# Two-layer graph network on one core: sweep 2 rearranged (halves, one more tile place, a fixed order of TensorE's steps), weights requested later, features transposed in pairs of blocks

## The chip, the cores and the metric

The kernel runs on one core of a Trainium2 chip. The metric is the device time of one execution in microseconds (us); the times of the kernel before are the median of three runs. A profile is one execution recorded by the hardware profiler: its span goes from the first to the last instruction of the program, and the time of that same execution is somewhat longer than its span.

## The reference

`x` is 4096 x 64, `adj` is 4096 x 4096 with about 0.8% of its entries set and the diagonal added. Two layers follow each other, each with a layer norm and a ReLU in front and a residual around it:

```python
h = relu(layernorm(x))                       # layer 0
for k in range(2):                           # two hops
    agg = adj @ h
    h = tanh(concat([agg, h], axis=1) @ W[k])
x = x + h
h = relu(layernorm(x))                       # layer 1
support = h @ weight
mask = adj != 0
rank = cumsum(mask, axis=1); deg = rank[:, -1:]
k = minimum(deg, 100)
pos = rank - (deg - k)
w = mask * where(pos > 0, 0.5 ** (k - pos), 0)
x = x + (w @ support + bias)
```

So `adj` is multiplied three times by a 4096 x 64 matrix: twice in float32 by its values, and once by weights 0.5^(k - pos) that follow from the running count of non-zero entries in each row.

## The kernel before, in words

The 4096 nodes are four chunks of eight blocks of 128. `adj` arrives transposed. TensorE works on tiles of 128 x 1024 entries: one source block against one chunk of destinations. Since the features are 64 wide, the two 512-wide halves of a tile go to two column halves of the array at the same time (`agg_pair`, L302). Each float32 matmul leaves two records in the trace, so one such tile is four records.

**Sweep 1** (L479 on) reads all of `adj` once, in pairs of blocks of 1 MB, and does hop 1, all four chunks of destinations one after the other; chunk 0 comes first, with an order of its own (L568). While a tile lies in SBUF, VectorE and ScalarE also turn it into running counts, one byte an entry, that stay in SBUF as `codes` (L267 to L287). `features_T` (L316) transposes a chunk's normalized features, `weighted` (L226) multiplies them with the upper half of W[0] ahead of the hop, `own_share` (L240) with the lower half. One array `hx` holds both, features in its first 64 columns and weighted features in the last 64. `at_step` says after which tile of chunk 0 each of these calls stands. As soon as a chunk has its hop-1 result, it is put in the place of its features, and the tiles of later rows that touch it serve hop 2 as well: those tiles are multiplied twice (`fused`). These 1 MB tiles are counted from 0 in the order of their loads (0 to 15 belong to chunk 0), the half-MB tiles of sweep 2 from 0 again. Of row 1, the pairs with blocks 3 and 1 are moved behind its first EARLY = 7 pairs. SyncE issues all loads; each waits for its place to come free (`places`, `busy`, `load`, L509).

**Sweep 2** (`sweep2`, L931) loads the remaining 72 half-MB tiles of `adj` a second time, for the part of hop 2 that sweep 1 could not do (`hop`, L976; L987 for chunk 0), in the order of `plan`: chunk 2, chunk 3, the rest of chunk 2, chunk 1, chunk 0. When a chunk's hop-2 sum is there, `finish_x2` (L679) takes it through the product with W[1] (`py`, L697), Tanh, residual, layer norm and ReLU, and writes the layer-1 features as a high and a low part in `feat` (L743, L744). Layer 1 is 128 units (J, g, n): source chunk J, destination chunk g, block n. A unit needs the features of chunk J and one 128 x 1024 tile of weights, which `convert` (L790) makes from the codes: on ScalarE with one Exp (L810), or on VectorE with two operations through a buffer `bits` (L802, L805). `layer1` (L856) then does two full-width matmuls (L870). Sums of a (J, g) that are not `kept` in PSUM are added to `parts` in SBUF (`evict`, L887). `finish_out` multiplies a destination chunk with the layer-1 weight (`pto`, L918), adds bias and residual and writes it out.

The order in which the engines get their instructions is fixed when the program is built, by a planner in `sweep2`: it keeps a clock for each engine with estimated durations (`use`), lets the converters run ahead of TensorE by `lead`, and at each point chooses whether the next thing on TensorE is a unit or a tile, by which tiles it believes to have landed and how many units can run. `n_late` = 56 units are held back until the tiles are through. The places of weights come from `space`: buffers that are free again, such as ring pairs that need no more tiles (`consumed`, `KEEP` = 4 of five ring pairs go on), and the codes of a (J, g) that is done (`pair_space`). Tiles of sweep 2 have the ten places of the ring and, once, the place of `hx0`.

Each engine works through its own queue in order and waits on semaphores.

Of the kernel before, what the change touches and what calls it, by code (L numbers as in the profile page):

```python
# [44 lines left out]
def gnn_kernel(  # L45
# [50 lines left out]
    hxs = [place([P, CB, 2 * D], F32, f"hx{q}", "hx") for q in range(NCH)]  # L96
    at = lambda b: hxs[b // CB][:, b % CB, :]
# [129 lines left out]
    def weighted(I):  # L227

        v = by_t(flat(pre1[:, chunk(I), :]))
        pt = (one if I % 2 else two)(name="pg")  # L230
        for t in range(TC):
            nc.tensor.matmul(  # L232
                pt[:, t * P : (t + 1) * P].rearrange("p (c e) -> p c e", c=NC),
                v[:, t // 2, t % 2, :], wz[:, :, 0, 0, :],
                start=True, stop=True, skip_group_check=True,
            )
        nc.scalar.copy(
            as_nodes(hxs[I][:, :, D:]), pt.rearrange("p (t c e) -> p t c e", t=TC, c=NC)
        )

    def own_share(I, po=None):

        h = flat(pre1[:, chunk(I), :])
        keep = po is not None
        po = po if keep else two(name="po")
        paired(po, (lambda c: wz[:, c, 0, 1], lambda c: h), last=not keep)
        if not keep:
            nc.scalar.copy(h, po)
# [69 lines left out]

    def features_T(I):

        pt = (two if I % 2 else one)(name="ph")
        for t in range(TC):
            for c in range(NC):
                nc.tensor.matmul(
                    pt[c * D : (c + 1) * D, t * P : (t + 1) * P],
                    hxs[I][:, c * TC + t, :D], ident, start=True, stop=True, skip_group_check=True,
                )
        nc.scalar.copy(
            by_t(flat(pre1[:, chunk(I), :])), pt.rearrange("q (u v p) -> q u v p", u=2, v=2)
        )  # L330
# [49 lines left out]
    def finish_first(acc, quads):  # L380
# [4 lines left out]
        def x1_half(c):  # L385
# [14 lines left out]
            for h in range(2):  # L400
                nc.scalar.copy(
                    as_nodes(hxs[0][:, :, :D])[:, 2 * h : 2 * h + 2, c], nodes(banks[h])[:, :, 0, c]
                )

        def hop1(b):
            for c in range(NC):
                nc.tensor.matmul(  # L407
                    G[c * D : (c + 1) * D, :], at(b)[:, :D], part_of(quads[c, b // 4], b),
# [33 lines left out]
    def finish_row(I, acc):  # L442
# [9 lines left out]
        take(hxs[I][:, :, :D], banks, 0)  # L452
# [26 lines left out]
    def sweep1():  # L479
        b0 = NB - CB // 2  # L480
        load_x(NCH - 1)
        first = ln_relu(hxs[-1][:, CB // 2 :, :D], pre1[:, b0:, :])
        NQ = NB // 4
        order1 = {I: [*range(NB - 1, 0, -2)] for I in range(1, NCH)}
        EARLY = 7
# [44 lines left out]
        MARKS1 = (6, 9, 12, 15)  # L530
        marks0 = {1: 2, 2: 4, 7: 8, 10: 13, 11: 15}
        F, G, S = features_T, weighted, own_share
        at_step = {1: [(F, 3), (F, 2)], 2: [(G, 3), (G, 2)], 4: [(S, 2)], 5: [(F, 0)], 6: [(G, 0)], 7: [(F, 1)], 8: [(G, 1)], 9: [(S, 3)], 10: [(S, 1)]}
        to_count = [*range(8), *range(9, 16), 8]

        for k in range(2 * NQ):
            _, (c, q) = units[k]
            if k == 0:
                load(1)
                load_x(2)  # L540
                copies = load_weights()
                next(copies)
                load(2)
                load_x(1)
                load(3)
                load_x(0)
            if k == 1:
                next(copies)
# [3 lines left out]
            if k == 0:  # L552
                rest = ln_relu(hxs[-1][:, : CB // 2, :D], pre1[:, NB - CB : b0, :])
                for g in (2, 1, 0):
                    lns[g] = ln_relu(hxs[g][:, :, :D], pre1[:, chunk(g), :])
                ends = []
                for n in (CB // 2, 0):
                    v = slice(n, n + CB // 2)
                    ends.append(ln_relu(hxs[2][:, v, :D], pre1[:, 2 * CB :, :][:, v]))
                for g in (first, first, rest, first, rest, ends[0], rest, ends[0], ends[1], ends[0], ends[1]):  # L560
                    next(g, None)
# [4 lines left out]
            for b in (4 * q + n for n in (2, 3, 0, 1)):  # L566
                h = b % 2
                nc.tensor.matmul(  # L568
                    low0[c][h * D : (h + 1) * D, :], at(b)[:, :D], part_of(a, b),
# [3 lines left out]
            order_ = {0: (1, 2), 1: (1, 'n', 1), 2: (0,), 3: (0, 0)}.get(k, ("n", "n") if k == 7 else ("n",))  # L573
# [24 lines left out]
        for k in range(2 * NQ, len(units)):  # L598
# [16 lines left out]
            for r in (1, 0):  # L615
                g = b - 1 + r
                last = n == HB - 1 and r == 0
                agg_pair(acc[1], at(g)[:, D:], a[:, r], g == NB - 1, last)
# [485 lines left out]
```

## Time and profile before

| what | value |
|---|---|
| time, median of 3 runs (lowest, highest) | 341.48 us (340.38, 344.35) |
| the profiled execution: time, span | 343.04 us, 341.3 us |
| TensorE matmul busy | 329.6 us |
| VectorE busy | 280.4 us |
| ScalarE busy | 190.5 us |
| moved by DMA, mean rate | 108.47 MB, 318 GB/s |
| granted TensorE clock | 1.000 |
| stages, by TensorE: first tile; tile 6; end of hop 1 (first tile of sweep 2 after it); first unit; tiles of sweep 2 through; last matmul | 6.9; 26.6; 196.7; 223.7; 301.6; 337.7 us |

A line of instructions in the profile names the source line, the engine, the operation, what is written and read, the shape and the number of instructions; then come busy time, the mean of one in ns, and idle time before them with what ended it. In the timeline a line begins with start and duration in us and ends with the idle time ahead of it in brackets. PE is TensorE, PEld its weight loads, DVE VectorE, ACT ScalarE, POOL GpSimd, SP SyncE. The clock column of the profile stays at full speed throughout.

### The profile page before, as it was taken

The numbers are of one execution on the slowest core, as the hardware profiler recorded it, in microseconds if no ns is written. First come the engines' busy times: TensorE is split into PE (matmuls) and PEld (weight loads), VectorE is DVE, ScalarE is ACT, GpSimd is POOL, SyncE is SP. The second block draws the span as 40 slices with busy tenths as digits, with TensorE's granted clock in tenths as the row PEclk, the third lists the DMA queues.
The fourth block names the chain that finished last, engine by engine and source line by source line (L and its number), as shares of the span: only waits on it lengthen the run. The fifth ranks groups of instructions, "written<-read, shape, count | busy, mean of one in ns | idle before, by whom it ended". The sixth has DMA issues, their size and how long they took to land.

```text
span 341.3 us, 4305 instructions
## 1 busy us (share of the span) xinstructions
PE 329.6 (97%) x1578; PEld 150.1 (44%) x1578; DVE 280.4 (82%) x439; ACT 190.5 (56%) x199; POOL 23.5 (7%) x21
## 2 busy tenths in 40 slices
PE   8699999999999999999999999899999999998995
PEld 2354433433334333343333433143454656466885
DVE  4869999999999999999969683779456799889933
ACT  2493673285444590233480424037468999969990
POOL 2340000000000000000000000312003000003000
PEclk9999999999999999999999999999999999999999
DMA  7999999999999889976999999999996946500012
GB/s 265 420 423 420 424 415 427 418 422 421 421 418 423 371 321 419 356 270 219 381 361 292 324 356 411 409 409 407 407 396 237 344 151 219 198 17 0 2 52 71
DMA packets 22404, 108.47 MB, mean 318 GB/s; under 512 B 2416, under 2 KB 3824, under 8 KB 14320
## 3 DMA queue, kind: packets, MB, share of 16 engines
q1 hardware_dynamic: 22384, 108.21, 81.3%
q8 instruction: 12, 0.20, 0.2%
q14 instruction: 8, 0.07, 0.1%
HBM read 107.15 MB, written 1.05 MB: 317 GB/s over the span
## 4 chain that ended last, share of the span: by engine, by line
PE 82%; DMA 12%; DVE 3%; ACT 1%; SPq 0%; issue 0%
PE acc_low L302 25%; PE acc L302 20%; PE accl L870 16%; PE acc L987 6%; DMA codes<-in_adjA_dram 5%; DMA ring<-in_adjA_dram 5%; PE acc L568 4%; PE pto L918 2%; PE acc L407 2%; DMA wb<-in_weights_dram 2%; PE pt L370 2%; PE py L697 1%; PE acc_low L568 1%; PE po L215 1%; PE pg L232 1%; PE pt L396 1%
## 5 line engine op out<-in xcount | busy, mean ns | idle before, releaser
L810 ACT ACTIVATE weights<-codes 128x1024 fp32r<-128x1024 uint8 x91 | 87.6, 1044 | 7.0 <-PE accl L870 4.4
L302 PE MATMUL acc<-ring,hx 128*64 128x512 f32 x352 | 86.3, 597 | 1.7 <-DMA ring<-in_adjA_dram 1.7
L302 PE MATMUL acc_low<-ring,hx 128*64 128x512 f32 x264 | 65.5, 593 | 0.0
L870 PE MATMUL accl<-weights,feat 128*128 128x512 f32 x254 | 62.9, 399 | 1.5 <-DVE feat L744 1.5
L870 PEld LDWEIGHTS accl<-weights,feat 128*128 128x128 f32 x254 | 46.2, 188 | 20.7 <-ACT weights L810 7.1
L302 PEld LDWEIGHTS acc<-ring,hx 128*64 128x64 f32 x352 | 23.6, 136 | 52.5 <-issue 39.8
L471 DVE TENSOR_TENSOR codes<-codes,after 128x2048 uint16<-128x2048 uint16 x32 | 38.2, 1218 | 0.1
L302 PEld LDWEIGHTS acc_low<-ring,hx 128*64 128x64 f32 x264 | 19.0, 137 | 37.5 <-issue 37.4
L267 ACT ACTIVATE codes<-ring 128x2048 int8<-128x2048 f32 x10 | 19.1, 1908 | 27.7 <-DMA ring<-in_adjA_dram 27.6
L283 DVE TENSOR_SCALAR mbuf<-ring 128x2048 uint8<-128x2048 f32 x28 | 34.2, 1221 | 0.0
L268 ACT ACTIVATE codes<-codes 128x2048 uint8<-128x2048 int8 x17 | 32.5, 1910 | 0.5
L276 DVE TENSOR_SCALAR cnt<-codes 128x1024 uint16<-128x1024 uint16 (+1 forms) x80 | 29.9, 373 | 2.7
L275 DVE TENSOR_TENSOR codes<-mbuf,cnt 128x1024 uint16<-128x1024 uint16 (+1 forms) x51 | 30.0, 588 | 1.9
L805 DVE TENSOR_SCALAR weights<-bits 128x1024 fp32r<-128x1024 f32 x36 | 25.9, 719 | 6.1 <-PE accl L870 2.2
L302 PE MATMUL acc_low<-codes,hx 128*64 128x512 f32 x120 | 27.8, 593 | 0.0
L802 DVE TENSOR_SCALAR bits<-codes 128x1024 uint32<-128x1024 uint8 x36 | 24.9, 691 | 0.8
L718 POOL TENSOR_TENSOR pre<-pre,wb 128x512 f32<-128x512 f32 x4 | 5.4, 1360 | 270.3 <-DVE xc L197 260.6
L987 PE MATMUL acc<-ring,hx 128*64 128x512 f32 x96 | 21.9, 598 | 0.0
L283 DVE TENSOR_SCALAR mbuf<-codes 128x2048 uint8<-128x2048 f32 x17 | 20.7, 1220 | 0.0
L202 POOL TENSOR_TENSOR s<-s,half 128x8 f32<-128x8 f32 (+1 forms) x10 | 16.9, 1688 | 18.2 <-DVE s L201 18.2
L275 DVE TENSOR_TENSOR codes<-codes,cnt 128x1024 uint16<-128x1024 uint16 (+1 forms) x24 | 13.9, 580 | 3.7 <-ACT codes L268 2.4
L302 PEld LDWEIGHTS acc_low<-codes,hx 128*64 128x64 f32 x120 | 8.5, 137 | 17.0 <-issue 17.0
(98 smaller groups left out, 275.4 us busy)
## 6 DMA issues: line engine op xcount, KB each, us to landing
ring<-in_adjA_dram SPq DMA_DIRECT2D x74, 512.0 KB, 7.9
ring<-in_adjA_dram SPq DMA_DIRECT2D x37, 1024.0 KB, 8.2
codes<-in_adjA_dram SPq DMA_DIRECT2D x26, 1024.0 KB, 17.7
pre<-in_x_dram SPq DMA_DIRECT2D x4, 256.0 KB, 6.9
xres<-in_x_dram SPq DMA_DIRECT2D x4, 256.0 KB, 8.7
out_dram<-o SPq DMA_DIRECT2D x3, 256.0 KB, 2.5
out_dram<-o SPq DMA_DIRECT2D x2, 128.0 KB, 2.2
wb<-in_weights_dram SPq DMA_DIRECT2D x1, 192.0 KB, 6.3
```

Of the source, the lines that this page charges most:

```text
L267: nc.scalar.activation(sign, tile_of(I, a), AF.Sign)
L268: nc.scalar.activation(m, sign, AF.Square, scale=float((FLAG - 1 + 0.25) ** 0.5))
L275: nc.vector.tensor_tensor(q, m, cnt, op=ALU.add)
L276: nc.vector.tensor_scalar(cnt, q, 0x7F7F, None, op0=ALU.bitwise_and)
L283: nc.vector.tensor_scalar(m, tile_of(I, a), 0.0, float(FLAG - 1), op0=ALU.not_equal, op1=ALU.mult)
L302: nc.tensor.matmul(acc[c * D : (c + 1) * D, :], src, a[:, c * C : (c + 1) * C], start=first, stop=last,)
L471: nc.vector.tensor_tensor(q, q, a[:, None, :].to_broadcast([P, 4, CW // 2]), op=ALU.subtract)
L802: nc.vector.tensor_scalar(state["bits"], q, float(ZERO), ONE, op0=ALU.subtract, op1=ALU.mult)
L805: nc.vector.tensor_scalar(w, state["bits"].bitcast(F32), 2.0 ** (127 - LOW), None, op0=ALU.mult)
L810: nc.scalar.activation(w, q, AF.Exp, scale=LN2, bias=BIAS)
L870: nc.tensor.matmul(sums[g][:, c, :], feats[J][:, k, :], w[:, c * C : (c + 1) * C], start=first, stop=last,)
L987: nc.tensor.matmul(accs[0][c * D : (c + 1) * D, :], at(b + h)[:, :D], tiles[n + c][2][:, h * C : (h + 1) * C], start=(0, b + h) == firsts[ ...
```

## The change

It has three groups of edits.

*Start and sweep 1.* The load of the layer weights is issued after that of tile 1 instead of before it, and their copy into place (`W`) is a call in `at_step`; the pieces of the layer norms stand in another order on VectorE (`'frffrarbaab'`, `order_`). `hx` is split into `hx` (features) and `gx` (weighted features), each with two chunks in one array. Chunks 1 to 3 are transposed by four 128 x 128 transposes of two adjacent blocks each, instead of eight matmuls with the identity; `weighted` and `own_share` follow the new order of columns. `own_share(3)` moves from step 9 to 8, `weighted(1)` from 8 to 9, `own_share(1)` from 10 to 11. EARLY is 10 instead of 7. Row 1 gets one more mark on ScalarE, one settle moves from (2, 9) to (3, 2), and the marks of two tiles of chunk 0 move.

*Places.* `gx1` is a twelfth place for tiles of sweep 2, requested ahead of the ring's; `gx0` takes the part that `hx0` had. Three instead of four ring pairs go on, and the pairs in `tile_pairs` become places for tiles when their codes are used. `bits` gets two buffers from unit 32 on, and VectorE can convert two units in one go.

*Sweep 2.* `plan` takes two blocks of chunk 2 ahead of chunk 3 instead of four. `finish_x2` works in two halves for chunks 3 and 0 (`SPLIT`), with the copy of the sum shared between ScalarE and VectorE; a unit waits for the half of the features that it reads, and the blocks of a unit group are ordered by halves. `kept`, `order` and `in_low` change which sums stay in PSUM: three (J, g) are spilled instead of eight. The choice by estimated landing is replaced by `steps2`: after so many tiles, so many units.

```diff
-    hxs = [place([P, CB, 2 * D], F32, f"hx{q}", "hx") for q in range(NCH)]
+    hxs, gxs = (
+        [v[:, q] for r in range(NCH // 2) for v in [place([P, 2, CB, D], F32, f"{n}{r}", n)] for q in range(2)]
+        for n in ("hx", "gx")
+    )
...
     def features_T(I):
...
+        if I:
+            for j in range(CB // 2):
+                nc.tensor.transpose(pair(pt, j), pair(flat(hxs[I]), j), ident)
+            nc.scalar.copy(h, pt)
+            return
...
-        EARLY = 7
+        EARLY = 10
...
-        at_step = {1: [(F, 3), (F, 2)], 2: [(G, 3), (G, 2)], 4: [(S, 2)], 5: [(F, 0)], 6: [(G, 0)], 7: [(F, 1)], 8: [(G, 1)], 9: [(S, 3)], 10: [(S, 1)]}
+        at_step = {1: [(W, 0), (F, 3), (F, 2)], 2: [(G, 3), (G, 2)], 4: [(S, 2)], 5: [(F, 0)], 6: [(G, 0)], 7: [(F, 1)], 8: [(S, 3)], 9: [(G, 1)], 11: [(S, 1)]}
...
-                load(1)
-                load_x(2)
                 copies = load_weights()
-                next(copies)
-                load(2)
-                load_x(1)
-                load(3)
-                load_x(0)
-            if k == 1:
-                next(copies)
+                ask = {"w": lambda: next(copies), "t": lambda: load(len(tiles) + 1)}
+                ask.update((str(q), partial(load_x, q)) for q in range(NCH))
+                for v in 't2tw1t0':
+                    ask[v]()
...
-                for g in (first, first, rest, first, rest, ends[0], rest, ends[0], ends[1], ends[0], ends[1]):
-                    next(g, None)
+                parts = {"f": first, "r": rest, "a": ends[0], "b": ends[1]}
+                for g in 'frffrarbaab':
+                    next(parts[g], None)
...
-            order_ = {0: (1, 2), 1: (1, 'n', 1), 2: (0,), 3: (0, 0)}.get(k, ("n", "n") if k == 7 else ("n",))
+            order_ = {0: (1, 2), 1: ('n', 1), 2: (0, 1, 0), 3: (0,)}.get(k, ("n", "n") if k == 7 else ("n",))
...
     def finish_x2(I, acc):
...
+        split = I in SPLIT
+        parts = [slice(0, 1), slice(1, 2)] if split else [slice(0, 2)]
+        tiles = [slice(2 * u.start, 2 * u.stop) for u in parts]
...
+        for a in tiles:
+            b = slice(2 * a.start, 2 * a.stop)
+            nc.vector.tensor_tensor(nodes_(y[:, b]), sums_[:, a], x2[:, a], op=ALU.add)
+            t = use("DVE", 0.7 * size, p + 0.2)
+            nc.scalar.activation(y[:, b], y[:, b], AF.Tanh)
+            t = use("ACT", 0.65 * size, t + 0.1)
...
-    order = {3: (0, 1, 2, 3), 2: (3, 0, 1, 2), 1: (2, 3, 0, 1), 0: (0, 1, 2, 3)}
-    kept = {(3, 3), (2, 2), (1, 0), (1, 1)}
-    units = [(J, g, n) for J in range(NCH - 1, -1, -1) for g in order[J] for n in range(CB)]
+    order = {3: (0, 1, 2, 3), 2: (1, 2, 3, 0), 1: (2, 3, 0, 1), 0: (1, 0, 2, 3)}
+    spilled = {(3, 0), (2, 1), (1, 2)}
+    kept = {(J, g) for J in range(1, NCH) for g in range(NCH)} - spilled
+    in_low = {(3, 2), (1, 1), (0, 2)}
+    units = [
+        (J, g, n) for J in range(NCH - 1, -1, -1) for g in order[J] for n in (0, 1, 4, 5, 2, 3, 6, 7)
+    ]
+    SPLIT = {0, 3}
...
-        KEEP = 4
+        KEEP = 3
+        GX = 50
+        steps2 = [(22, 9), (29, 14), (34, 19), (39, 22), (46, 33), (50, 41), (56, 61), (72, 128)]
...
-        plan = [(2, 16, 20), (3, 24, 32), (2, 20, 32), (1, 16, 32), (1, 8, 16), (0, 8, 32)]
+        plan = [(2, 16, 18), (3, 24, 32), (2, 18, 32), (1, 16, 32), (1, 8, 16), (0, 8, 32)]
...
+        load(1, 0, place([P, CW], F32, "gx1", "ring"), -20.0)
         for n, k in enumerate(rings):
...
-            elif go == 1:
-                layer1()
-            elif go == 2:
-                n += hop(n)
+            elif n < to[0] and n + (not blocks[n][0]) < len(tiles):
+                n += hop(n)
+            elif i < to[1] and half_of(units[i]) in ready and (len(made) > i or spaces):
+                layer1()
```

## Prediction

> **What bounds the kernel now.** I read the busy line, the chain that ended last, TensorE's waits, then TensorE's timeline of sweep 2, because sums hide stages with different limits.
>
> ```profile
> PE 329.6 (97%) x1578; PEld 150.1 (44%) x1578; DVE 280.4 (82%) x439; ACT 190.5 (56%) x199; POOL 23.5 (7%) x21
> ...
> PE 82%; DMA 12%; DVE 3%; ACT 1%; SPq 0%; issue 0%
> ```
>
> TensorE is nearly always busy, so only its own work, its waits and the ends of the program can give time. The chain in order of time (start, duration) says where DMA holds it:
>
> ```profile
> 8.86 17.71 DMA codes<-in_adjA_dram
> 26.61 1.94 PE acc_low L568 x8
> ```
>
> Until 26.6 us the DMA queue sets the end: adjacency tile 6 lands at 26.57. After it TensorE runs without a wait until 191. TensorE's waits (total, times, longest):
>
> ```profile
> PE acc_low L568 <- DMA ring<-in_adjA_dram: 2.6, 1, 2.6
> PE acc L302 <- DMA ring<-in_adjA_dram: 1.7, 8, 0.3
> ...
> PE accl L870 <- DVE feat L744: 1.5, 1, 1.5
> ```
>
> The second line understates: a matmul's modelled end lies past the point where the next could start. The timeline (start, busy, then idle before) shows the spacing:
>
> ```profile
> 217.93 1.08 PE L302 MATMUL acc<-ring,hx 128*64 128x512 f32 x4 [0.20 <-DMA ring<-in_adjA_dram]
> 219.21 1.08 PE L302 MATMUL acc<-ring,hx 128*64 128x512 f32 x4 [0.20 <-DMA ring<-in_adjA_dram]
> ...
> 223.74 0.73 PE L870 MATMUL accl<-feat 128*128 128x512 f32 x2
> ...
> 238.20 3.65 PE L302 MATMUL acc<-ring,hx 128*64 128x512 f32 x16
> 241.78 2.68 PE L870 MATMUL accl<-weights,feat 128*128 128x512 f32 x10
> 244.39 5.37 PE L302 MATMUL acc<-ring,hx 128*64 128x512 f32 x24
> 249.69 2.11 PE L870 MATMUL accl<-weights,feat 128*128 128x512 f32 x8
> ...
> 264.22 3.94 PE L870 MATMUL accl<-weights,feat 128*128 128x512 f32 x16
> 268.09 1.94 PE L987 MATMUL acc<-ring,hx 128*64 128x512 f32 x8
> ...
> 286.97 5.78 PE L870 MATMUL accl<-weights,feat 128*128 128x512 f32 x24
> 292.67 8.95 PE L987 MATMUL acc<-ring,hx 128*64 128x512 f32 x40
> ...
> 315.35 7.54 PE L870 MATMUL accl<-weights,feat 128*128 128x512 f32 x32 [1.54 <-DVE feat L744]
> ```
>
> A half-MB tile is four records, a layer-1 unit two. Start to start, 24 tile records took 5.30 us and 16 took 3.58, so a tile costs 0.86 and a group of tiles 0.14 more. 24 unit records took 5.70 and 16 took 3.87: a unit costs 0.457 and a group of units 0.21 more. One alternation of the two kinds costs 0.35. Waiting for DMA, tiles came 1.28 apart.
>
> Sweep 2's head, from its first tile after the last row of sweep 1 (196.69) to the first unit (223.74), is 27.05 us for 24 tiles (20.6) and two product groups `py` (1.15 each, counted 2.3): 4.1 lost to DMA. The other loss is 1.54 us, plus about 0.15 of restart, for the features of chunk 0.
>
> The converters of codes to weights also run near full speed late:
>
> ```profile
> 274.05 26.63 ACT L810 ACTIVATE weights<-codes 128x1024 fp32r<-128x1024 uint8 x28
> ```
>
> That is 0.951 us each on ScalarE; VectorE's pair of operations took 1.4 to 1.5.
>
> **What the Trainium skill says.** "TensorE: Matmul & The Clock Gate", Terms, gives the transpose mode as four times faster for FP32, and "TensorEngine Tiling (Array Packing)", Restrictions, says column tiling disables it. The trace agrees only that today's column-tiled product with the identity runs as ordinary matmuls: 16 records, 0.87 us a chunk in steady flow. It shows no transpose mode. "DMA: Bandwidth & Descriptors", Bandwidth, puts the ceiling near 436 GB/s; the trace reaches 414 to 424 when many tiles are queued, but 240 to 350 between 176 and 200 us, where tiles are released two at a time. "VectorE: DVE Perf Modes", the TRN2 errata section, describes a fixed cost per instruction: here 0.69 us for 128x512 and 0.42 for 128x256, so a half costs 61%.
>
> **Start and sweep 1.** Weights (192 KB) move behind tile 1 on SyncE's queue; the tile lands about 0.5 earlier, the weights near 11.4, wanted by ScalarE's copies at 14.5; but tile 6 has the same bytes ahead of it and lands near 26.6, so this and the faster transposes of chunks 3 and 2 gain nothing on the path. The new order of normalization pieces puts the counting of tile 0 (2.65) ahead of chunk 1's second half, so its features arrive near 21.0 instead of 18.9; tile 4 may wait 0.9, again before tile 6. Chunk 1's transpose comes after tile 6: four full transposes for eight column-tiled products. Unknown cost: below 0.2 (a quarter of 0.87), above 1.14 (what `weighted`'s four full-width matmuls take). I take 0.42: gain 0.45, range -0.3 to +0.65. Moving `weighted(1)` one tile later removes its 0.3 wait for ScalarE at 35.8. The 256-wide halves of `own_share` stream the same columns: 0, or 0.1 each worse. Sweep 1 gives **0.75**.
>
> At nothing: split hx/gx arrays (same reads); EARLY 10 (tile 26 lands at 76.3, wanted about 79.9; 3.6 us of cover); one more mark on ScalarE, idle there between 72 and 96; moved settles.
>
> **Head of sweep 2.** A twelfth tile slot (`gx1`) is free from about 169 and its load stands ahead of the ring's, where DMA has gaps; tile n then lands when n-1 did, less the 0.75. Tile 13 landed at 206.39 before, so about 204.5 now, then one per 1.28, tile 21 at 214.8. TensorE starts at 195.95: ten tiles, `py`, ten tiles would end at 214.3; the last waits to 214.8 and ends at 215.65. Lost 1.35 instead of 4.1: **2.75** gained; range 1.3 (the slot fills no gap) to 4.1.
>
> Units start after 20 tiles, not 24. Chunk 3's features must be there by 215.65. Its sum ends at 202.8, two tiles sooner in order. In halves: copy 0.37, first half of `py` at 205.2, add, Tanh, residual add, reduce, centre at 0.42 each to 207.75, the second half's three interleaved to 209.1, Square, reduce, power on GpSimd 1.01 (four columns at the start; eight took 2.56), then scale and split: half 0 near 212, half 1 near 213. Slack 2.6 to 3.6. VectorE's queued settles (1.22 each) stand behind both halves. Six weight buffers exist then, so unit 8's conversion follows unit 3's matmul by 2.9: 0.2 lost.
>
> **Fixed steps.** Eight groups of units for twelve: 4 x 0.35 = **1.4**. 67 units instead of 56 are left when the tiles end. TensorE takes its queue in order, so a group that waits for a weight, a feature or a tile holds everything behind it, as it did before.
>
> DMA: three ring pairs kept plus `gx1` make 7 places, then 9 (pair of unit 16) and 8. With 1.28 each, tile 33 lands at 230.8 (wanted 233.5), tile 45 near 246.5 (wanted 248); later margins exceed 3.
>
> **Tail.** From 215.65: 50 tiles 42.9, 61 units 27.9, two `py` 2.1, seven alternations 2.5, conversion waits 0.5; tiles end at X = 291.5. Chunk 0's chain in halves gives its first features at X + 10.6; before it took 13.6 after 301.6. The first unit of chunk 0 is now preceded by 35 units, at X + 17.1. The **1.7** goes. Next late is ScalarE: 94 conversions for 92 (VectorE 34 for 36), and after the second Square (X + 6.1) it owes 29 and a copy. The conversion for unit 109 ends at X + 23.0, wanted X + 23.0 + 0.7; the last at X + 34.3, wanted X + 34.9. It fits by 0.6. VectorE's pairs fit by 0.6 to 3, helped by 12 sum operations instead of 20 (8 x 0.65 = 5.2, off the path). Small conversion waits inside before's units, some 0.6, I leave in after too. The halves add some ten VectorE operations a chain (0.42 + 0.42 for 0.69, about 1.5 us for each of two chunks), behind which only conversions queue; the bias sum on GpSimd (1.36) now follows the powers and is read only by the output.
>
> Sum: 0.75 + 2.75 + 1.4 + 1.7 = 6.6. The profiled span of 341.3 becomes 334.7, that execution 343.04 becomes 336.4. The median of the runs, 341.48, lies 1.56 below the profiled execution; the prediction on the median is 334.9.
>
> **Rivals.**
> - Conversions take over. The margin of 0.6 is thin, and the Tanh and Square halves make ScalarE wait four times where it waited twice. If it stands 3 us longer, the end moves 2.4: 337.3. For it: 26.63 us without a gap already. Against: buffers fill while 16 tiles run without units.
> - Head and sweep 1 give nothing: the early slot takes DMA time from the ring instead of a gap, and the transpose costs what it did. 0.75 + 1.3 lost: 337.0. For it: DMA's busy share is 0.9 to 1.0 from 176 to 200. Against: its rate is 240 to 350 there, not 414.
> - Slower: with 7 places the DMA queue runs shallow and tiles come at the pace of 197 to 201, 2.0 us. Between 215.65 and 256 the fixed order needs 26 tiles in 40.3 us of TensorE work (22.4 + 33 units 15.1 + 1.15 + 5 x 0.35), 1.55 each; above that each tile delays all. At 2.0: 26 x 0.45 = 11.7, and 346.6. Against: with eight places it held 1.28.
>
> **Numbers.** Forecast 0.63 (332.5 to 336.5), conversions 0.16, nothing at the head 0.13, slower 0.07, the rest 0.01. Range 332.5 to 339: from no DMA wait at all to the first two rivals with two more us. One per cent, 3.4 us, is about what this measurement can tell from no change. Below 338.1: forecast and most of the first two rivals, 0.84; within: 0.09; above: 0.07.
>
> **What would show it.** First unit near 215.7 after 20 tiles; no wait of `accl` for features; eight groups; one transpose chunk under 0.6; first tile of sweep 2 near 196. I am wrong if units wait for weights by more than 1.5 in the last 43 us, tiles wait for DMA after 220, or chunk 3's features come after 215.7.

## The result, and the profile after

Over six runs each on one chip the changed kernel took 337.76 us (median, 336.97 to 339.36) and the kernel before 342.89 (340.38 to 344.35): the ratio is 0.985, 95% interval 0.982 to 0.989. Two more comparisons, in the experiments below, gave 0.990 (0.987 to 0.994) and 0.987 (0.983 to 0.992). The forecast was 334.9 with a range of 332.5 to 339.0. The sign and the range held; the gain is 5.1 us where 6.6 were worked out, and the time lies above the band that the prediction gave to the forecast itself (332.5 to 336.5).

The profiled execution took 337.74 us (span 336.0) against 343.04 (span 341.3). Its busy line and the engine shares of its chain:

```profile
PE 325.8 (97%) x1554; PEld 150.1 (45%) x1554; DVE 273.4 (81%) x445; ACT 195.4 (58%) x206; POOL 22.1 (7%) x23
...
PE 90%; DMA 5%; DVE 2%; ACT 1%; SPq 0%; POOL 0%; issue 0%; ACTq 0%; POOLq 0%
```

DMA's share of the chain fell from 12% to 5%. The bound is still TensorE, and it stands idle less. What TensorE waits for after the change (total, times, longest):

```profile
PE acc_low L582 <- DVE s L204: 2.3, 1, 2.3
PE pw L167 <- DVE warm L169: 1.5, 1, 1.5
PE ph L338 <- DVE hx L208: 1.2, 1, 1.2
PE accl L945 <- ACT weights L860: 0.4, 2, 0.2
PE acc L313 <- DMA ring<-in_adjA_dram: 0.4, 2, 0.2
```

The feature wait of 1.5 us is gone, and so are all eight tile waits, which stood ahead of the first unit; two new ones stand near 248 us. New are also a wait of the transposes (`ph`) for normalized rows, and two waits for weights. The first line is the old wait for tile 1, 2.6 us before, under another name: tile 1 landed at 11.50, 0.13 us ahead of its first matmul, as in the kernel before (11.36 and 11.49). The second, for the warm-up, was there before with 1.4. L313 is the old L302, L945 the old L870, L1092 the old L987. In the timeline of sweep 2 (start, busy, idle before) the new waits have these places:

```profile
196.47 8.80 PE L313 MATMUL acc<-ring,hx 128*64 128x512 f32 x40
...
206.34 8.90 PE L313 MATMUL acc<-ring,hx 128*64 128x512 f32 x40
215.17 0.73 PE L945 MATMUL accl<-feat 128*128 128x512 f32 x2
...
219.01 0.73 PE L945 MATMUL accl<-weights,feat 128*128 128x512 f32 x2 [0.21 <-ACT weights L860]
219.96 0.73 PE L945 MATMUL accl<-weights,feat 128*128 128x512 f32 x2 [0.22 <-ACT weights L860]
220.62 4.51 PE L313 MATMUL acc<-ring,hx 128*64 128x512 f32 x20
...
243.65 4.58 PE L313 MATMUL acc<-ring,hx 128*64 128x512 f32 x20
248.42 1.08 PE L313 MATMUL acc<-ring,hx 128*64 128x512 f32 x4 [0.20 <-DMA ring<-in_adjA_dram]
249.70 1.08 PE L313 MATMUL acc<-ring,hx 128*64 128x512 f32 x4 [0.20 <-DMA ring<-in_adjA_dram]
...
278.98 13.95 PE L1092 MATMUL acc<-ring,hx 128*64 128x512 f32 x64
292.87 1.20 PE L945 MATMUL accl<-weights,feat 128*128 128x512 f32 x4
```

Read the starts, not the idle figures. From 196.47 to 215.17 are 18.70 us for 20 tiles and one `py`, which cost 18.35 at the known prices: the head loses 0.35 where it lost 4.1. The first group of nine units lasts 215.17 to 220.62, 5.45 us, where nine units and a change of kind cost 9 x 0.457 + 0.21 = 4.32: 1.1 us are lost to two conversions. Five tiles from 243.65 should be through at 247.95; the sixth starts at 248.42 and the seventh at 249.70 instead of 249.28: 0.9 us lost to tiles.

The late tiles have stood in a queue that ran low earlier. The stretch from 215 to 232 us in the kernel before (busy time of each engine with its instructions, clock, DMA share and, last, GB/s):

```profile
215.00:232.00 17.00, 15.91 (x70) 5.78 (x70) 12.70 (x17) 4.80 (x6) 4.78 (x3) 1.00 1.03 409
```

The same stretch in the changed kernel:

```profile
215.00:232.00 17.00, 16.57 (x74) 8.30 (x74) 12.69 (x18) 9.49 (x12) 1.31 (x2) 1.00 0.89 330
```

While nine units run, no tile is consumed, so no place comes free: SyncE issues a tile at 215.28 and the next at 221.74. Landings at 223.67 and 225.34 are followed by one at 228.86. A second pause of the issues, from 228.19 to 231.68, goes with landings at 236.48 and 239.30. In the kernel before, landings between 222 and 242 us are 1.1 to 1.4 apart.

To compare kernels, distances from the first tile of sweep 2 behind the last row (T0) serve best, because T0 itself moves from one execution to the next (the twelve traces here that share the changed sweep 1 have it between 195.52 and 196.87). The last column is the start of the last product group `pto`.

| kernel | T0 | first unit | last `pto` | ratio of times (95%) |
|---|---|---|---|---|
| before | 196.69 | +27.05 | +137.12 | 1 |
| after, three traces | 196.47, 195.80, 195.63 | +18.70, +18.61, +19.06 | +131.97, +132.79, +131.87 | 0.985, 0.990, 0.987 |
| e1 no place, new order | 195.57 | +22.12 | +137.78 | 1.003 (1.000 to 1.007) |
| e2 no halves | 196.04 | +20.42 | +133.77 | 0.993 (0.990 to 0.995) |
| e3 halves of chunk 3 alone, 56 units left | 196.66 | +18.60 | +134.31 | 0.993 (0.991 to 0.996) |
| e4 old order of normalization | 196.29 | +18.97 | +133.10 | 0.984 (0.975 to 0.992) |
| e6 place, old order | 195.74 | +25.00 | +133.07 | 0.992 (0.989 to 0.994) |
| e7 three more groups | 195.88 | +18.61 | +133.00 | 0.990 (0.985 to 0.995) |
| e8 first group of 7 | 196.87 | +18.83 | +133.20 | 0.992 (0.989 to 0.995) |
| e9 no place, old order | 196.09 | +27.04 | +138.89 | 1.004 (1.002 to 1.007) |
| e10 nine places | 195.52 | +18.60 | +138.18 | 1.008 (1.006 to 1.010) |
| e11 first group of 5 | 196.15 | +18.61 | +132.02 | 0.988 (0.984 to 0.992) |

### The profile page after: what moved, and what is told of

It reads as the page before. It is cut to its first block, busy times and chain, and to the rows that moved or that the text cites. A ratio compares the mean times of both kernels' runs of the same rounds, so it can differ in the third digit from the quotient of the medians.

```text
span 336.0 us, 4283 instructions
## 1 busy us (share of the span) xinstructions
PE 325.8 (97%) x1554; PEld 150.1 (45%) x1554; DVE 273.4 (81%) x445; ACT 195.4 (58%) x206; POOL 22.1 (7%) x23
## 3 DMA queue, kind: packets, MB, share of 16 engines
HBM read 107.15 MB, written 1.05 MB: 322 GB/s over the span
## 4 chain that ended last, share of the span: by engine, by line
PE 90%; DMA 5%; DVE 2%; ACT 1%; SPq 0%; POOL 0%; issue 0%; ACTq 0%; POOLq 0%
PE acc_low L313 25%; PE acc L313 22%; PE accl L945 17%; PE acc L1092 6%; PE acc L582 4%; PE acc_low L582 3%; DMA ring<-in_adjA_dram 3%; PE pto L1003 2%; DMA pre<-in_x_dram 2%; PE acc L424 2%; PE pt L387 2%; PE py L719 1%; PE pg L235 1%; PE po L254 1%; PE pt L413 1%; ACT weights L860 1%
## 5 line engine op out<-in xcount | busy, mean ns | idle before, releaser
L313 PE MATMUL acc<-ring,hx 128*64 128x512 f32 x352 | 84.7, 596 | 0.4 <-DMA ring<-in_adjA_dram 0.4
L313 PE MATMUL acc_low<-ring,gx 128*64 128x512 f32 x264 | 65.5, 593 | 0.0
L945 PE MATMUL accl<-weights,feat 128*128 128x512 f32 x250 | 61.2, 397 | 0.4 <-ACT weights L860 0.4
L945 PEld LDWEIGHTS accl<-weights,feat 128*128 128x128 f32 x250 | 45.8, 188 | 16.5 <-ACT weights L860 5.9
L313 PEld LDWEIGHTS acc<-ring,hx 128*64 128x64 f32 x352 | 24.2, 137 | 49.5 <-issue 44.4
L870 DVE TENSOR_SCALAR weights<-bits 128x1024 fp32r<-128x1024 f32 x33 | 22.1, 691 | 17.0 <-PE accl L945 9.0
L313 PEld LDWEIGHTS acc_low<-ring,gx 128*64 128x64 f32 x264 | 19.0, 137 | 37.5 <-issue 37.1
L279 ACT ACTIVATE codes<-codes 128x2048 uint8<-128x2048 int8 x18 | 34.4, 1910 | 0.6
L313 PE MATMUL acc_low<-codes,gx 128*64 128x512 f32 x120 | 27.7, 593 | 0.0
L865 DVE TENSOR_SCALAR bits<-codes 128x1024 uint32<-128x1024 uint8 x34 | 22.7, 687 | 0.1
L768 POOL TENSOR_TENSOR s<-s,half 128x4 f32<-128x4 f32 (+1 forms) x6 | 8.2, 1370 | 221.7 <-DVE s L764 221.7
L1092 PE MATMUL acc<-ring,hx 128*64 128x512 f32 x96 | 21.2, 594 | 0.0
L278 ACT ACTIVATE codes<-codes 128x2048 int8<-128x2048 f32 x8 | 15.2, 1905 | 3.2 <-DMA codes<-in_adjA_dram 3.2
L224 ACT COPY x1T<-acc 64x512 f32<-64x512 f32 x6 | 3.5, 579 | 22.1 <-PE acc L313 22.1
```

What stands on the lines that cost most here:

```text
L278: nc.scalar.activation(sign, tile_of(I, a), AF.Sign)
L279: nc.scalar.activation(m, sign, AF.Square, scale=float((FLAG - 1 + 0.25) ** 0.5))
L313: nc.tensor.matmul(acc[c * D : (c + 1) * D, :], src, a[:, c * C : (c + 1) * C], start=first, stop=last,)
L865: nc.vector.tensor_scalar(bits[k - n], q, float(ZERO), ONE, op0=ALU.subtract, op1=ALU.mult)
L945: nc.tensor.matmul(sums[g][c], feats[J][:, k % TC * NC + k // TC, :], w[:, c * C : (c + 1) * C], start=first, stop=last,)
L1092: nc.tensor.matmul(accs[0][c * D : (c + 1) * D, :], at(b + h), tiles[n + c][2][:, h * C : (h + 1) * C], start=(0, b + h) == firsts[0], sto ...
```

## The experiments

**The twelfth tile place taken away (e1).**

```diff
-        load(1, 0, place([P, CW], F32, "gx1", "ring"), -20.0)
...
             if n in (1, 3, 5):
                 next(last, None)
+            if n == GX:
+                space(place([P, CW], F32R, "gx1", "weights"), clock["PE"] + 0.2)
```

> The changed kernel without the twelfth tile place: gx1 takes no tile and becomes a weight buffer at the same point as before. Theory (the place is filled in a DMA gap, every tile lands 1.28 us earlier): the 22nd tile of sweep 2 lands at about 215.4 instead of 214.1, TensorE waits for tiles by 1.0 to 1.3 us more before the first unit, first unit at 216.2 to 216.5 instead of 215.2, the tiles of sweep 2 are through 0.6 to 1.2 us later. Rival (the slot takes its time from the ring's tiles, no gain): first unit within 0.3 us of 215.2.

Measured: 343.27 us, the time of the kernel before (342.55 in the same comparison). The whole gain is gone. Waits of TensorE:

```profile
PE acc L313 <- DMA ring<-in_adjA_dram: 3.1, 9, 0.8
```

Seen from T0 the first unit is 3.1 to 3.5 us later, where 1.0 to 1.3 were expected, and the last product 5.0 to 5.9. The place does more than move each landing up by one: the last tile of the head is requested at 209.14, behind a pause of 6.4 us in SyncE's loads, and lands at 216.64; in the changed kernel it is requested at 203.60 and lands at 214.12. After the first unit the kernel again lacks tiles (three of the nine waits), and its tail is 1.3 us longer, with waits of the last products for the copied sums; the cause of this last part is open. Note what this edit does to the number of places. The changed kernel keeps `KEEP = 3` pairs of the ring for tiles once the head is through, and `gx1` beside them, seven places; the kernel before kept four pairs, eight. Without `gx1` only six are left, fewer than before. So e1 is not "the kernel before in the head"; it is a point with six places. The edit also hands `gx1` to the weights some tiles later than the changed kernel does; no unit waits for a weight after the first group, so this did not hold up TensorE.

**The halves taken away (e2).**

```diff
-    SPLIT = {0, 3}
+    SPLIT = set()
```

> The changed kernel with no chunk in halves in sweep 2. Theory (the halves matter at the first unit alone): the whole chain of chunk 3 gives features near 216.3, so TensorE stands about 1.2 us at the first unit; the tail keeps its length of 39.5 us from the last tile to the last matmul, since chunk 0's features come 13.6 us after it and are wanted 17 after. In all 1.2 to 2.0 us slower than the changed kernel. Rival (the halves remove the tail's stall): TensorE waits over 1 us for features in the tail.

Measured: 339.93 us. All of it is one wait, ahead of the first unit, in the timeline:

```profile
216.46 0.74 PE L945 MATMUL accl<-feat 128*128 128x512 f32 x2 [1.55 <-DVE feat L791]
```

From T0 the first unit comes 1.4 to 1.8 us later. From the last tile (294.10) to the last `pto` (329.81) are 35.71 us against 35.57: in the tail the halves of chunk 0 give nothing. What the halves give, they give at chunk 3.

**Halves of chunk 3 alone, and 56 units left at the end instead of 67 (e3).**

```diff
-        steps2 = [..., (56, 61), (72, 128)]
+        steps2 = [..., (56, 61), (64, 72), (72, 128)]
...
-    SPLIT = {0, 3}
+    SPLIT = {3}
```

> The changed kernel with 56 instead of 67 units left after the last tile (11 units between tiles 64 and 65) and halves for chunk 3 alone. Theory (the stall of 1.5 us went because 35 units, not 24, precede chunk 0's first one): the stall for features comes back with 1.5 to 2.0 us, one alternation costs 0.35 more; 1.9 to 2.4 us slower than the changed kernel. Rival (the spilled sums taken off VectorE make chunk 0's features early): no stall, 0.4 us slower.

Measured: 339.93 us, and the wait of the kernel before is back in the timeline, with 1.12 us for 1.54 (1.5 to 2.0 were expected):

```profile
312.04 7.50 PE L945 MATMUL accl<-weights,feat 128*128 128x512 f32 x32 [1.12 <-DVE feat L791]
```

So the tail's stall has two cures, more units left over or a shorter chain, and either alone removes it: e2 has the first, e6 below the second.

**The old order of normalization pieces and counting (e4).**

```diff
-                for g in 'frffrarbaab':
+                for g in 'ffrfrarabab':
...
-            order_ = {0: (1, 2), 1: ('n', 1), 2: (0, 1, 0), 3: (0,)}...
+            order_ = {0: (1, 2), 1: (1, 'n', 1), 2: (0,), 3: (0, 0)}...
```

> The changed kernel with the order of normalization pieces and of the calls between tiles 0 to 3 as before the change. Theory (the new order brings chunk 2's features 1.1 us later to its transpose, and TensorE, not DMA, then comes late to tile 6): TensorE's wait at the transposes falls from 1.24 to under 0.4, sweep 2 starts 0.4 to 0.8 us earlier than 196.5. Rival (DMA sets the start in any order): tile 6 is computed within 0.2 us of 26.8 and sweep 2 starts at 196.3 to 196.6.

Measured: 337.06 us, six runs, ratio 0.984 with a wide interval. The timeline of the start has the transposes of chunks 3 and 2 in one piece, without the 1.2 us wait for rows that the changed kernel has there:

```profile
11.28 3.00 PE L582 MATMUL acc_low<-ring,hx 128*64 128x512 f32 x8 [2.19 <-DMA ring<-in_adjA_dram]
14.22 1.66 PE L338 MATMUL ph<-ident,hx 128*128 128x128 f32 x8
15.81 1.94 PE L582 MATMUL acc_low<-ring,hx 128*64 128x512 f32 x8
```

But the same trace has another reason for this: in this one execution the granted clock was down here (columns as above, the clock third from the end), and tile 1 took 3.00 us for 1.94:

```profile
12.00:16.00 4.00, 4.00 (x16) 1.92 (x14) 3.48 (x9) 1.72 (x4) 1.06 (x2) 0.57 1.01 422
```

The other traces have a clock of 1.00 there. At their pace TensorE would have come to chunk 2's transposes near 13.7 (an estimate: 11.28, 1.87 for tile 1 and 0.58 for four transposes), and the rows were written at 14.49, so part of the wait would be left. The tile behind the transposes starts at 15.81 instead of 15.99. T0, 196.29, is inside the changed kernel's own spread. What the two orders differ by can't be told from the times, nor from a trace with a lower clock: neither the theory nor the rival is decided.

**The changed kernel again (e5), as a mark for e6 to e8.**

> The changed kernel itself once more, as the mark for the other three on this chip. Ratio to the kernel before 0.985 (0.982 to 0.989), so about 5 us less. If the two waits for tiles near 248 us (0.2 us each in the records) come from the fixed order, they come again; if they were an accident of one execution, they are absent or elsewhere.

Measured: 338.37 us. The two weight waits came at the same places in the order and with the same size. The tile waits came too, but bigger: one at 240.93 (0.66 us by its start), then 0.74 and 0.42 at 248.57 and 249.85, 1.8 us in all against 0.9 in the first trace; the third trace (e12) has 0.4 after the first unit. All three traces of this order have late tiles near 248 us, so they come with the order; why their size differs from one execution to the next no run shows.

**The place and the halves kept, the order of before (e6).**

```diff
-        steps2 = [(22, 9), (29, 14), (34, 19), (39, 22), (46, 33), (50, 41), (56, 61), (72, 128)]
+        steps2 = [(26, 3), (30, 5), (33, 7), (36, 10), (40, 15), (46, 19), (48, 28),
+                  (54, 36), (56, 48), (60, 60), (62, 72), (72, 128)]
```

> The changed kernel with the order of tiles and units that the kernel before had (24 tiles before the first unit, twelve groups of units, 56 units left for the end). Theory, that the extra tile place is what pays and the fixed steps only add their alternations: four more alternations cost 1.4 us and nothing else is lost, so 1.4 us above the changed kernel and about 3.6 us below the kernel before; the head has no tile wait, first unit near 196.5 + 20.6 + 2.3 = 219.4, no wait for the features of chunk 0. Rival, that place and steps only pay together: within 1 us of the kernel before, 4 to 5 us above the changed kernel, with tile waits that come back between 225 and 260 us.

Measured: 339.17 us against e5's 338.37; the intervals overlap. Seen from T0 the last product is 0.3 to 1.2 us later than in the three traces of the changed kernel. Four alternations more cost 1.4 at the known price; against that no unit waits for a weight, and after the head one tile waits. TensorE's waits for tiles:

```profile
PE acc L313 <- DMA ring<-in_adjA_dram: 1.3, 3, 1.0
```

Two of these three are in the head, where 24 tiles are wanted before the first unit: 25.00 us for work of 22.9, a loss of 2.1 where none was expected. Of the 5 us that the change gives, the new order accounts for about one at most. With 56 units left and chunk 0 in halves there is no feature wait.

**More groups (e7).**

```diff
-        steps2 = [..., (39, 22), (46, 33), (50, 41), (56, 61), (72, 128)]
+        steps2 = [..., (39, 22), (43, 27), (46, 33), (50, 41), (52, 47), (54, 54), (56, 61), (72, 128)]
```

> The changed kernel with four more groups of units and of tiles (three of the groups of tiles cut in five more pieces, less one that falls together with a group that was there), everything else in the same order. Theory, 0.35 us an alternation: 1.4 us above the changed kernel. Rival, that the cost of an alternation is hidden in the pipeline: less than 0.5 us. Below the changed kernel if the shorter groups close the tile waits near 248 us (0.8 us).

The trace shows eleven groups of units, three more than the eight of the changed kernel, not four as the expectation counted; at 0.35 each that is 1.05 us. Measured: 337.71 us, ratio 0.990, no loss to be seen in the times. The trace separates it. From the start of the five tiles after the units of 234 us to the start of the last 16 tiles:

```profile
236.95 3.65 PE L313 MATMUL acc<-ring,hx 128*64 128x512 f32 x16
241.21 1.08 PE L313 MATMUL acc<-ring,hx 128*64 128x512 f32 x4 [0.60 <-DMA ring<-in_adjA_dram]
...
279.42 13.96 PE L1092 MATMUL acc<-ring,hx 128*64 128x512 f32 x64
```

That is 42.47 us, less 0.82 for the late tile (wanted at 236.95 + 4 x 0.86 = 240.39), 41.65. The same stretch in the three traces of the changed kernel is 41.36, 42.30 and 40.88, less tile waits of 0.89, 1.82 and 0.42: 40.47, 40.48 and 40.46. Three alternations cost 1.18, 0.39 each. The price of 0.35 was right to within 0.04. The two late tiles near 248 us are gone and one at 241 us is there, as in e5; that shorter groups let places come free more evenly is a reading that fits, not one that this run shows.

**A first group of seven units, and eleven units moved ahead of two tiles (e8).**

```diff
-        steps2 = [(22, 9), (29, 14), (34, 19), (39, 22), (46, 33), ...]
+        steps2 = [(22, 7), (29, 14), (34, 19), (39, 22), (44, 33), ...]
```

> The changed kernel with two of its steps moved: the first group of units has 7 units and the second 7 (9 and 5 in the changed kernel), and the 11 units that come after tile 46 come after tile 44. Theory, that the changed kernel loses 0.9 us to conversions in its first group of units and 0.8 us to tiles near 248 us: 1.0 to 1.7 us below the changed kernel, one wait for a weight in the first group where there were two, no tile wait before the 11 units. Rival, that the conversions or the tiles are then late elsewhere: the same time within 0.5 us, with the waits at another place.

Measured: 339.38 us, not faster. No tile waits, and no weight in the first group, but the timeline has them later:

```profile
230.61 0.73 PE L945 MATMUL accl<-weights,feat 128*128 128x512 f32 x2 [1.35 <-ACT weights L860]
231.56 0.72 PE L945 MATMUL accl<-weights,feat 128*128 128x512 f32 x2 [0.21 <-ACT weights L860]
...
239.51 0.73 PE L945 MATMUL accl<-weights,feat 128*128 128x512 f32 x2 [0.74 <-ACT weights L860]
```

The waits are at another place, as the rival had it; whether the time is within its 0.5 us the intervals leave open (from T0 the last product is 0.3 to 1.3 us later). The second group now has seven units for five, and its sixth and seventh are the ones that wait. Their conversions stand in ScalarE's queue behind the Square of chunk 2:

```profile
228.98 0.63 ACT L748 ACTIVATE sq<-xc 128x512 f32<-128x512 f32 x1 [2.69 <-DVE xc L744]
229.52 4.83 ACT L860 ACTIVATE weights<-codes 128x1024 fp32r<-128x1024 uint8 x5
```

Whether a buffer was free earlier no run shows.

**No twelfth place, and the old order (e9).**

The edits of e1 and e6 together.

> The changed kernel without the twelfth tile place and with the order of tiles and units of the kernel before: what is left of the change is the halves, the transposes, the start and the split arrays. It closes the square of place and order. Measured so far from the first tile of sweep 2 to the start of the last product: 137.1 us in the kernel before, 137.8 with the new order and no place, 133.1 with the old order and the place, 132.0 and 132.8 with both. Theory, that the place is worth about 2.4 us in the old order and 5.4 in the new one, and that the halves alone take away the 1.7 us for the features of chunk 0: 135.4 here, about 1.7 us less than the kernel before in time, first unit 27 us after the first tile. Rival, that the place is worth 5 us in any order: 138, the time of the kernel before.

Measured: 343.80 us, 0.4% slower than the kernel before. The theory fell: +138.89 from T0 where it gave 135.4, and the rival's number came out: the place is worth 5.8 us in the old order (138.89 less 133.07) and 5.0 to 5.9 in the new one. The head is as expected, +27.04, that of the kernel before to 0.01: in the old order the place gives the head 2.0 us. The rest, 3.8 us over e6, is lost after the first unit. TensorE's waits for tiles:

```profile
PE acc L313 <- DMA ring<-in_adjA_dram: 4.7, 11, 1.3
```

Five of these eleven waits lie between 234 and 252 us, where the kernel before had none and e6 has one; by the starts they lose 3.2 us. Two waits for weights near 261 us lose 0.9 more. The kernel before had eight places there, e6 has seven, e9 has six. That is what the slower rival of the prediction describes, a DMA queue that runs shallow, and it is there at six places.

**Nine places, and two weight buffers fewer (e10).**

```diff
-        KEEP = 3
+        KEEP = 4
```

> The changed kernel with one more pair of tile places kept for tiles until tile 18 or so of sweep 2 (9 places where it has 7), and so two buffers fewer for weights. Theory, that the tile waits near 241 and 248 us come from too few places while the first group of units runs: those waits are gone (0.8 to 1.4 us gained), and the first group of 9 units waits for four weights instead of two, 0.5 us each (1 us lost), so the same time within 0.7 us. Rival, that the tile waits come from the rate of the DMA queue: they stay, and the time is 1 us longer.

Measured: 344.96 us, 0.8% slower than the kernel before, where I had expected to break even. No tile waits are left. The first group takes 7.35 us (214.12 to 221.47), 3.0 lost, and the next stalls again. TensorE's waits for conversions (total, times, longest):

```profile
PE accl L945 <- ACT weights L860: 3.3, 7, 2.0
PE accl L945 <- ACT feat L860: 0.5, 2, 0.3
```

The longest of them in the timeline:

```profile
232.59 1.20 PE L945 MATMUL accl<-weights,feat 128*128 128x512 f32 x4 [2.01 <-ACT weights L860]
```

Two buffers fewer cost 5.4 to 6.3 us from T0 to the last product, of which 1.3 us are the longer tail that e1 had too. A pair of the ring is two tile places or two weight buffers, and at this point both are short.

**Shorter first groups (e11), and the changed kernel beside it (e12).**

```diff
-        steps2 = [(22, 9), (29, 14), (34, 19), (39, 22), (46, 33), (50, 41), (56, 61), (72, 128)]
+        steps2 = [(22, 5), (27, 8), (32, 12), (37, 17), (43, 24), (49, 33), (56, 48), (62, 64), (72, 128)]
```

> The changed kernel with other fixed steps: after the same 20 tiles only 5 units (no more than there are weight buffers), then groups of 3, 4, 5, 7, 9, 15 and 16 units between groups of 5 to 7 tiles; nine groups for eight. Theory, that the long first group of units starves both sides (conversions by 0.9 us, tiles by 0.8 to 1.4): both waits gone, one more alternation, 1.0 to 1.5 us below the changed kernel. Rival, that the waits only move to later groups, as they did when the first group had 7 units: the time of the changed kernel within 0.5 us.

> The changed kernel as the mark for the other three on this chip: 0.985 to 0.990 of the kernel before; 132.0 to 132.8 us from the first tile of sweep 2 to the start of the last product.

Measured: 337.99 us for e11 and 337.67 for e12. In e11 no unit waits for a weight any more, and DMA moves 390 GB/s between 215 and 232 us where the changed kernel moved 330 (columns as above):

```profile
215.00:232.00 17.00, 17.00 (x78) 8.16 (x79) 12.93 (x15) 10.64 (x13) 3.40 (x2) 1.00 1.01 390
```

One tile wait of 0.52 (at 242.88) remains, the last `py` waits 0.42 for its sum, and there is an alternation more. From T0 to the last product it is 132.02, like the changed kernel. The waits were exchanged for others of about the same size, as the rival had it. No version here beats the changed kernel beyond what the times can tell.

Some edits were not taken back alone: which sums stay in PSUM, the pairs of codes that become tile places, the second buffer of `bits`, the split arrays and the other edits of sweep 1. What each of them is worth is open.

## Why the prediction was right, and where it was not

**Direction and bound.** TensorE was the bound and stayed it; the gain is time that TensorE no longer waits, and 1.4 us of alternations. That held, and the largest term, the head, was named as such. In the first pair of traces the terms are 3.8 at the head, 1.4 for alternations and 1.7 in the tail, less 1.1 lost to conversions and 0.9 to late tiles: 4.9 of the 5.15 us that the last product came nearer to T0.

**Start and sweep 1, 0.75 forecast.** Half of it is there. T0 was 196.69 in the one trace of before and 195.63 to 196.47 in three of after. From TensorE's start on tile 6 to T0 are 170.08 us in the kernel before and 169.69 to 169.70 in the three traces after: 0.38 gained. Ahead of tile 6 the difference changes with the execution. The step that failed there is "tile 6 ... lands near 26.6, so this and the faster transposes of chunks 3 and 2 gain nothing on the path". Tile 6 landed at 25.73 and TensorE reached it at 26.77, busy without a break since the new wait at the start, as the timeline shows:

```profile
15.40 0.66 PE L338 MATMUL ph<-ident,hx 128*128 128x128 f32 x4 [1.24 <-DVE hx L208]
15.99 1.94 PE L582 MATMUL acc_low<-ring,hx 128*64 128x512 f32 x8
...
32.46 0.66 PE L338 MATMUL ph<-ident,hx 128*128 128x128 f32 x4
33.04 1.94 PE L582 MATMUL acc<-codes,hx 128*64 128x512 f32 x8
```

The start hangs on chunk 2's normalized rows now, and these on the load of its rows of `x`, with which the chain that ended last begins:

```profile
2.11 6.87 DMA pre<-in_x_dram
...
14.93 0.43 DVE hx L208
```

In ten of the twelve traces that share this start, T0 is 187.5 us behind the landing of that load, which came between 8.15 and 9.40 us. So a load still decides the start, but another one. Chunk 1's transposes took 0.58 us (32.46 to 33.04) for 0.87, but began 0.1 later behind the product ahead of them: from tile 6 to chunk 1's next tile 0.24 gained, not 0.45, inside the bounds given. The price that was unknown is 0.145 us for one FP32 transpose of 128x128. The column-tiled product that it replaces took 0.87 for 16, and so the four-fold gain for FP32 that the Trainium skill states ("TensorE: Matmul & The Clock Gate", Terms) came out as a factor of 1.5 for the step; the old form already ran as column-tiled pairs, which may be why, but no run separates that. From chunk 1's next tile (33.12 before, 33.04 after) to T0 are 163.57 and 163.43 us: 0.14 gained, where 0.3 had been worked out for `weighted(1)`.

**Head, 2.75 forecast.** Right in mechanism, too small by 1.0: the first unit came 18.7 us behind T0 where 19.7 were worked out. The term mis-sized is the landing of the tiles. Tile 13 was put 8.55 us behind T0 and came 6.2 to 7.8 behind it in the three traces, so more than one landing was gained; the last tile, put at 214.8, landed at 214.12, and 0.35 was lost instead of 1.35. By e6 and e9 the place alone gives 2.0 in the old order, by e1 it gives 3.1 to 3.5 in the new one, both inside the bounds of 1.3 and 4.1. Chunk 3's features needed the halves: without them they were 1.55 late (e2). With them the halves were written at 212.93 and 215.15, 2.2 us before the first unit and 2.0 before the fifth, the first to read the second half; the second half had been put near 213.

**Fixed steps, 1.4 forecast.** The alternation was priced rightly (0.39 by e7) and eight groups came. The steps that failed stand beside it: "unit 8's conversion follows unit 3's matmul by 2.9: 0.2 lost", and "tile 45 near 246.5 (wanted 248)"; tile 45 landed at 249.66. From the first unit to the last tile 75.85 us were worked out and 77.70, 78.60 and 77.22 measured. The first group lost 1.1 to conversions, and tiles lost 0.4 to 1.8. I had costed landings at 1.28 apart throughout, without the 6.5 us in which nine units give no place back. Across that pause two tiles landed in 4.6 to 5.2 us in the three traces, for 2.6. That the pause is what makes tiles late 20 us on is a reading: in e11 it is 3.5 us long, and one tile is still 0.9 late. With this the order gives about one microsecond at most over the old one (e6), not 1.4.

**Tail, 1.7 forecast.** Right: no wait for features, and from the last tile to the end of the last matmul 39.6 us (X + 34.9, one unit and the last product make 39.3). ScalarE's thin margin of 0.6 held; no unit of the tail waits for a weight. The prediction named the halves of chunk 0 and the 35 units ahead of its first one together; the 67 units left over do it alone (e2), and so do the halves (e6).

**Rivals.** The first (conversions) was right that they are thin and wrong about where: in the first group, not in the tail. The second (nothing at the head) fell with e1 and e9. The third (shallow DMA) shows at six places (e1, e9); from seven on it is there in small, 0.4 to 1.8 us. With that one of the prediction's own signs of being wrong came true: tiles waited for DMA after 220.

**The rest of the miss.** In the profiled executions the sum gave 336.4 and 337.74 was measured, 1.3 apart: T0 came 0.5 later than worked out, the head was 1.0 shorter, the stretch from the first unit to the last tile 1.85 longer. That the head made good for part of the rest was luck, and so was a time in the zone of the first two rivals, which neither of them brought about. The other 1.5 us of the median is the offset: I took the median of three runs of before, 341.48, as the level, and its later comparisons lie at 342.0 to 342.9.

## What to carry to other kernels

When a buffer can serve two queues, count both sides at the tightest moment before pricing an edit: here one tile place decided between 338 and 343 us and two weight buffers between 338 and 345, while the visible edits (order, transposes, fewer alternations) were worth one to one and a half microseconds together. In this kernel long groups of one kind of work saved alternations but kept the other kind's buffers from coming free, and part of the saving went back into waits; look at what the DMA queue moved in that stretch, not at its mean. And undo a part only after checking what else depends on it: taking away the twelfth place also undercut a `KEEP` that had been lowered together with it.

## What the runs showed of the hardware that I had not expected

- An FP32 transpose of 128x128 took 0.145 us, only 1.5 times faster for a chunk than column-tiled products with the identity, 0.87 us.
- When only two tiles were still under way after a pause of 6.5 us in the issues, tiles issued 0.86 us apart, at 221.74 and 222.60, landed at 225.34 and 228.86, and only then came 1.28 apart: 3.6 us, then 6.3 us, from issue to landing.
- The rows that the second transposes wait for came between 14.50 and 15.59 us in four kernels with the same start (e1, e2, after, e3), and T0 followed: half a microsecond up or down is decided by the landing of a load of `x` near 9 us.
- The same program lost 0.4, 0.9 and 1.8 us to late tiles after its first unit in three executions.
- In one execution of e4 the granted clock was 0.57 between 12 and 16 us and 1.00 in the other traces there; eight matmuls took 3.00 us for 1.94.
